# Decoder cells in a linear order beside each other, and channel gates made one chunk ahead of the routing

## The chip, the cores and the metric

The kernel runs on one core of a Trainium2 chip. A core has five engines with instruction streams of their own: TensorE (PE in the profile; its weight loads are listed apart as PEld), VectorE (DVE), ScalarE (ACT), GpSimd (POOL) and SyncE (SP), which mainly issues transfers. They work side by side and wait for each other through semaphores. The metric is the time of one execution on the device in microseconds (us), and of several executions the median.

## The reference

A tensor x of 8 sequences, 256 positions and 1024 features goes through three residual steps, each behind a layer norm. The first is a small decoder, which works at width 128 and has four layers; each layer is a recurrence along the 256 positions (written as a convolution by FFT in the reference) and a feedforward part. The second multiplies x by gates: for each sequence and feature, the 154 largest of 256 positions of a second input are marked, masked means and maxima over the positions are turned into gates by a 7-tap convolution, a batch norm and a sigmoid, and marked and unmarked positions get a gate each. The third is a mixture of 8 experts, two for each token. Cut to what matters (remarks behind # are added here):

```
def layernorm(x, w, b):                      # inside the decoder
    mu = jnp.mean(x, axis=-1, keepdims=True)
    var = jnp.mean((x - mu) ** 2, axis=-1, keepdims=True)
    return (x - mu) * jax.lax.rsqrt(var + EPS) * w + b
...
h = jnp.einsum('blv,dv->bld', x, Win) + bin  # 1024 -> 128
def body(h, p):                              # 4 layers
    l1w, l1b, pr, pi, lr, li, scl, l2w, l2b, w1, b1_, w2, b2_ = p
    y = jax.nn.silu(layernorm(h, l1w, l1b))
    y = sconv(y, pr + 1j * pi, lr + 1j * li) # complex exponential recurrence along the 256 positions
    h = h + y * scl
    y = layernorm(h, l2w, l2b)
    y = jax.nn.silu(jnp.einsum('bld,fd->blf', y, w1) + b1_)   # 128 -> 512
    y = jnp.einsum('blf,df->bld', y, w2) + b2_                # 512 -> 128
    return (h + y, None)
...
h = layernorm(h, lnl_w, lnl_b)
return jnp.einsum('bld,vd->blv', h, Wout) + bout              # 128 -> 1024
...
_, topk_idx = jax.lax.top_k(cm, k)           # k = 154 of 256, for each sequence and feature
mask = jnp.zeros((B, L, C), x.dtype).at[b_idx, l_idx, topk_idx].set(1.0)
...
return crucial_features * A_S1 + subcrucial_features * A_S2   # mask*x and (1-mask)*x, each gated
...
gate_logits = jnp.einsum('bsh,he->bse', x, gate_w)            # 8 experts
top_vals, top_idx = jax.lax.top_k(gate_logits, TOP_K)         # TOP_K = 2
...
expert_out = jnp.einsum('bsh,eho->bseo', x, expert_w)         # 1024 -> 1024
...
x = x + _L0_attn_ref(_layernorm(x, axis=-1), L0_attn_Win, ...
x = x + _L0_xattn_ref(_layernorm(x, axis=-1), ctx_4096, ...
x = x + _L0_ffn_ref(_layernorm(x, axis=-1), L0_ffn_gate_w, L0_ffn_expert_w)
return x
```

## The kernel before

The 2048 tokens are kept in the core's memory with features in the partitions, in four chunks (`NCH`) of 512 columns (`CT`), which are two sequences each. The kernel is written in Tile, a framework in which the program is plain Python and a scheduler fixes each engine's order of instructions when the kernel is built: it goes by the order in the program as priority, by what each instruction depends on, and by its own guess of durations, and may draw a later instruction ahead where an earlier one isn't ready by its guess. On the chip each engine then runs its list in that fixed order.

Five stages follow each other. **Decoder with threshold search** comes first. `start(c)` (L329 to L354) transposes a chunk (32 transposes, L337) for its statistics (L339) and multiplies it by Win (L348). A cell (l, c) is layer l for chunk c. Its first half is `recurrence` (L396 to L418): `inverse_std` squares on ScalarE (L382), sums by four narrow matmuls (L385), adds epsilon on VectorE (L388), takes the power on GpSimd (L390), and spreads it by four transposes (L137, in `over_features`); then VectorE normalizes (y, L399), ScalarE applies SiLU (L401), VectorE multiplies by the phases (mi, L405), runs four scans (L408) and multiplies again (L411), and TensorE adds the centered state (L413) and two matmuls with mi (L415) into one PSUM tile. Its second half is `feedforward` (L420 to L437): `inverse_std` on that tile, z on VectorE (L425), four matmuls with W1 (L429), four SiLUs on ScalarE (L432), four matmuls with W2 into the same PSUM tile (L435), and h on ScalarE (L437). After the last layer `put_out(c)` (L441 to L461) multiplies by Wout (eight matmuls, L458), adds to x (L459) and takes statistics for the next layer norm.

The order of cells is written at L464 to L504, in waves: wave w holds the cells with l + c = w, so that there are 1, 2, 3, 4, 3, 2 and 1 cells in the seven waves. All recurrences of a wave are written first, then the start of one more chunk, then all feedforwards of the wave:

```
cells = [(wave - c, c) for c in range(NCH) if 0 <= wave - c < DEPTH]
turned = [recurrence(l, c) for l, c in cells]
...
for (l, c), xc in zip(cells, turned):
    feedforward(l, c, xc)
```

The output weights are prepared in wave 3, and from that wave on each wave ends with `put_out`.

The search for the 154th largest value (L510 to L603) needs nothing from the decoder. It stands behind it in the program, so its instructions fill gaps. It has four parts of 16 rows: four trials of 16 Signs with a sum on ScalarE (L550), each followed by some nine small instructions on VectorE (L553 to L565); then for each of 16 rows three VectorE instructions (L571, L573, L574), small ones, and 16 comparisons that write the mask (L596). A branch (L606) for rows where the search failed follows; no engine goes past it before both the decoder and the search are done.

**Masked sums and maxima** (L632 to L650, VectorE and ScalarE) and **convolution and batch norm** (L679 to L750) come next. In **gating and routing** a loop over chunks (L893 to L908) makes four gates of four slices each on ScalarE (L902), adds the deviations and multiplies x on VectorE (L905, L907), and calls `route(c)` (L772 to L877): gate logits on TensorE (L779), transposes of the tokens to rows (L791), row statistics, normalized rows stored to memory, two experts picked of eight (sel, L826; wt, L827, L831), ranks within each expert (L839, L841), a payload (pay, L874) and eight scatters on GpSimd (L877). **Experts** comes last: the slots' tokens are gathered (L968), transposed (L940), multiplied by the expert's weights (L950), weighted and added into the output by indirect transfers (L991).

PSUM has three kinds of tiles of 128 x 512 in the decoder: tp in two buffers (transposes, W1 results, Wout results), mm in four (a cell's state), st in two (statistics). In the routing the pool is another one: st in two buffers and a tile of double size, x2, in two.

Of the kernel before, what the change touches and what calls it, by code (L numbers as in the profile page):

```python
# [8 lines left out]
F32 = mybir.dt.float32  # L9
# [6 lines left out]
P = 128  # L16
# [39 lines left out]
def decoder_kernel(ctx: ExitStack, tc: tile.TileContext, x_t, ctx_t, vecs, win_t, w1_t, w2_t, wout_t,  # L56
# [8 lines left out]
    until_gates = ctx.enter_context(ExitStack())  # L65
    psum = until_gates.enter_context(tc.tile_pool(name="psum", bufs=2, space=bass.MemoryType.PSUM))

    def ps_tp():
        return psum.tile([P, CT], F32, tag="tp", name="ps_tp", bufs=2)

    def ps_mm():
        return psum.tile([P, CT], F32, tag="mm", name="ps_mm", bufs=4)

    def ps_st():
        return psum.tile([P, CT], F32, tag="st", name="ps_st", bufs=2)


    ident = const.tile([P, P], F32, name="ident")
# [70 lines left out]
    with ExitStack() as early:  # L149
        tkp = early.enter_context(tc.tile_pool(name="topk", bufs=1))  # L150

        with ExitStack() as dec:
# [243 lines left out]
            def recurrence(l, c):  # L396
                rb = inverse_std(h[c])
                y = lp.tile([P, CT], F32, tag="y", name="y")
                nc.vector.tensor_tensor(y, h[c], rb, ALU.mult)  # L399
                s = lp.tile([P, 2, S], F32, tag="s", name="s")  # L400
                nc.scalar.activation(s.rearrange("p a t -> p (a t)"), y, AF.Silu,  # L401
                                     bias=col("ln1_b", l), scale=col("ln1_w", l))

                mi = lp.tile([P, 2, 2, S], F32, tag="mi", name="mi", bufs=2)
                nc.vector.tensor_tensor(mi, both(s, 1), both(turn[:, l], 2), ALU.mult)  # L405
                for a, ini in enumerate((init_a, init_b)):
                    for q in range(2):
# [3 lines left out]
                nc.vector.tensor_tensor(mi, mi, both(turn[:, l], 2), ALU.mult)  # L411
                xc = ps_mm()
                nc.tensor.matmul(out=xc, lhsT=center, rhs=h[c], start=True, stop=False)  # L413
                for a in range(2):
                    nc.tensor.matmul(out=xc, lhsT=turned_w[:, l],  # L415
                                     rhs=mi[:, a].rearrange("p q t -> p (q t)"),
                                     start=False, stop=(a == 1))
                return xc  # L418
# [22 lines left out]
            def put_out(c):  # L441
# [18 lines left out]
                                           ALU.add)  # L460
                wide_inverse_std(xs[c], inv_std[:, at_c])  # L461


            for wave in range(DEPTH + NCH - 1):  # L464
                cells = [(wave - c, c) for c in range(NCH) if 0 <= wave - c < DEPTH]
                turned = [recurrence(l, c) for l, c in cells]
                if wave == 0:
                    phases(slice(1, DEPTH))
                if wave + 1 < NCH:
                    start(wave + 1)  # L470
                for (l, c), xc in zip(cells, turned):
                    feedforward(l, c, xc)
                if wave == NCH - 1:

                    wo = wp.tile([P, NK, DIM], F32, tag="w_io", name="wo")
                    nc.sync.dma_start(out=wo.rearrange("p k d -> p (k d)"), in_=wout_t)
                    bp = ps_st()
                    for k in range(NK):
                        nc.tensor.matmul(out=bp[:, k : k + 1], lhsT=wo[:, k, :], rhs=col("lnl_b"), start=True,
                                         stop=True)  # L480
                    v.tensor_tensor(bo, bo, bp[:, 0:NK], ALU.add)
                    wo_mean = wp.tile([P, 1], F32, name="wo_mean")
                    v.tensor_reduce(wo_mean, wo, AX.XY, ALU.add)
                    v.tensor_scalar(wo_mean, wo_mean, 1.0 / D, None, ALU.mult)
                    v.tensor_scalar(wo, wo, wo_mean, col("lnl_w"), ALU.subtract, ALU.mult)
                    v.tensor_tensor(wo_mean, wo_mean, col("lnl_w"), ALU.mult)
                    bp = ps_st()
                    nc.tensor.matmul(out=bp[:, 0:NK], lhsT=mean_x, rhs=bo, start=True, stop=True)
                    bo_mean = wp.tile([P, 1], F32, name="bo_mean")
                    v.tensor_reduce(bo_mean, bp[:, 0:NK], AX.X, ALU.add)  # L490
                    v.tensor_scalar(bo, bo, bo_mean, None, ALU.subtract)


                    for g in range(2):
                        o = slice(4 * g, 4 * g + 4)
                        om = ps_tp()
                        nc.tensor.matmul(out=om, lhsT=ones, rhs=wo[:, o, :].rearrange("p k d -> p (k d)"),
                                         start=True, stop=True)
                        off = lp.tile([P, CT], F32, tag="z", name="off")
                        v.tensor_scalar(off, om, 1.0 / DIM, 1.0 / DIM, ALU.mult, ALU.add)  # L500
                        v.tensor_tensor(wo[:, o, :].rearrange("p k d -> p (k d)"),
                                        wo[:, o, :].rearrange("p k d -> p (k d)"), off, ALU.subtract)
                if wave >= DEPTH - 1:
                    put_out(wave - DEPTH + 1)  # L504

# [170 lines left out]
    with tc.tile_pool(name="xattn", bufs=2) as cp:  # L676
# [408 lines left out]
```

## Time and profile before

| | |
|---|---|
| time, median of 3 runs | 1357.23 us (1355.61 to 1359.68) |
| profiled execution, its own time | 1359.86 us |
| its span | 1358.0 us |
| mean granted TensorE clock | 0.862 |
| set-up and first start, 0 to 36.8 us | 36.8 us |
| decoder and search, to 503.7 us | 466.9 us, TensorE busy 366.4, VectorE 317.3, ScalarE 255.5 |
| masked sums and maxima, to 577.0 us | 73.3 us, VectorE busy 66.4 |
| convolution and batch norm, to 590.5 us | 13.5 us |
| gating and routing, to 731.8 us | 141.3 us, TensorE busy 79.7, VectorE 78.6, ScalarE 74.1 |
| experts, to 1358.0 us | 626.2 us, TensorE busy 597.5 |

The profile is one execution with its instructions' start and end times. The span is from the first to the last of them; the execution's own time has a little more around it. An instruction's row gives its line in the kernel, the engine, the operation, output and input tiles by their names in the program, and shapes. What ended an idle time is inferred from the semaphores. TensorE's granted clock is given as a share of full speed. A 128 x 512 matmul of 32-bit numbers shows as two records.

### The profile page before, as it was taken

Reading aid. Unit: us, or ns where it says so; the run is one execution under the profiler, and the core shown is the slowest. Engines: PE = TensorE matmul, PEld = TensorE weight load, DVE = VectorE, ACT = ScalarE, POOL = GpSimd, SP = SyncE. Lnnn points to the kernel's source line nnn. Section 1 sums busy time; section 2 is a strip of 40 time slices with the busy share of each in tenths; the row PEclk is TensorE's granted clock in tenths of the full one; section 3 lists DMA queues with packets and bytes.
Section 4 is the critical chain, followed back from the end, with each engine's and each line's share of the span. In section 5 each row is a group of like instructions: output and inputs, shape, how many; then the busy total and the mean of one; then the engine's idle time right before and its main releaser. Section 6 shows DMA issues by size and latency. Waiting matters only on the chain. (4 is left out here: it accounts for less than half of the span.)

```text
span 1358.0 us, 10519 instructions
## 1 busy us (share of the span) xinstructions
PE 1079.4 (79%) x3197; PEld 543.8 (40%) x3197; DVE 555.7 (41%) x1716; ACT 441.0 (32%) x1148; POOL 212.1 (16%) x213
## 2 busy tenths in 40 slices
PE   6778787987959661055663999999999999999996
PEld 4434344444434231023341444444444444444442
DVE  7771878387486769956651001000100010001000
ACT  0158565853847415956630000000000000000000
POOL 1021112101110010002323112111211112111100
PEclk9788787986979775557665999999999999999998
DMA  9100001001000000003375254362636253452622
GB/s 382 69 1 1 1 15 63 1 0 38 25 0 1 0 1 17 1 31 142 139 237 181 62 141 109 80 197 62 186 78 201 62 160 92 100 175 62 162 40 33
DMA packets 39203, 113.66 MB, mean 84 GB/s; under 512 B 4244, under 2 KB 4836, under 8 KB 37860
## 3 DMA queue, kind: packets, MB, share of 16 engines
q0 software_dynamic: 12544, 41.98, 14.3%
q1 hardware_dynamic: 23810, 62.44, 12.6%
q10 hardware_dynamic: 2786, 8.51, 1.6%
q8 instruction: 27, 0.44, 0.1%
q14 instruction: 36, 0.29, 0.1%
HBM read 74.57 MB, written 38.35 MB: 83 GB/s over the span
## 5 line engine op out<-in xcount | busy, mean ns | idle before, releaser
L950 PE MATMUL ps_mm<-w,xT 128*128 128x512 f32 x1280 | 561.2, 596 | 10.9 <-ACT xT L942 10.9
L950 PEld LDWEIGHTS ps_mm<-w,xT 128*128 128x128 f32 x1280 | 240.4, 190 | 308.2 <-issue 287.7
L990 DVE TENSOR_SCALAR y<-ps_mm,wgt 128x512 f32<-128x512 f32 x40 | 30.0, 751 | 544.5 <-PE ps_mm L950 530.9
L991 POOL DMA_INDIRECT out_dram<-y,to x40 | 63.1, 1577 | 497.3 <-DVE xT L944 415.7
L550 ACT ACTIVATE tkj<-ctx,tk_trial 128x256 f32<-128x256 f32 x256 | 129.1, 504 | 26.3 <-DVE tk_trial L565 17.1
L988 ACT ACTIVATE y<-ps_mm,wgt 128x512 f32<-128x512 f32 x40 | 27.5, 687 | 292.0 <-PE ps_mm L950 292.0
L942 ACT COPY xT<-ps_tp 128x512 f32<-128x512 f32 x40 | 23.4, 585 | 277.5 <-PE ps_tp L940 277.5
L390 POOL TENSOR_TENSOR rs<-ve,minus_half 128x4 f32<-128x4 f32 x36 | 42.5, 1182 | 245.5 <-DVE ve L388 223.6
L429 PE MATMUL ps_tp<-z,w 128*128 128x512 f32 x128 | 76.5, 726 | 3.5 <-DVE z L425 3.2
L415 PE MATMUL ps_mm<-mi,turned_w 128*128 128x512 f32 x64 | 48.8, 908 | 31.9 <-DVE mi L411 31.8
L137 PE MATMUL ps_st<-ident,rs 128*128 128x128 f32 x160 | 32.2, 333 | 41.0 <-POOL rs L390 41.0
L649 ACT ACTIVATE comb<-comb 128x256 f32<-128x256 f32 x128 | 51.5, 404 | 25.0 <-DVE smax L646 24.4
L435 PE MATMUL ps_mm<-f,w 128*128 128x512 f32 x128 | 59.4, 595 | 0.0
L432 ACT ACTIVATE f<-ps_tp,b1f 128x512 f32<-128x512 f32 x64 | 43.6, 683 | 27.4 <-PE ps_tp L429 26.9
L385 PEld LDWEIGHTS ps_st<-mean_w,sq 128*128 128x128 f32 x288 | 43.6, 228 | 11.7 <-ACT sq L382 7.3
L940 PEld LDWEIGHTS ps_tp<-ident,src 128*128 128x128 f32 x320 | 38.1, 143 | 25.5 <-issue 20.6
L550 ACT ACTIVATION_READ_ACCUMULATOR tkj<-ctx,tk_trial 128x1 f32 x256 | 48.1, 188 | 0.0
L940 PE MATMUL ps_tp<-ident,src 128*128 128x128 f32 x320 | 42.4, 276 | 4.8 <-DMA src<-normed_rows,to 4.8
L968 POOL DMA_INDIRECT src<-normed_rows,to x40 | 42.0, 1050 | 20.0 <-issue 11.6
L385 PE MATMUL ps_st<-mean_w,sq 128*128 128x1 f32 x288 | 42.2, 268 | 3.1 <-ACT sq L382 3.1
L429 PEld LDWEIGHTS ps_tp<-z,w 128*128 128x128 f32 x128 | 28.2, 233 | 40.0 <-issue 24.9
L877 POOL DMA_INDIRECT meta<-pay,at x32 | 34.4, 1074 | 59.8 <-DVE pay L874 51.2
(325 smaller groups left out, 1278.2 us busy)
## 6 DMA issues: line engine op xcount, KB each, us to landing
w<-in_expert_w_dram SPq DMA_DIRECT2D x32, 1024.0 KB, 7.6
x<-in_x_t_dram SPq DMA_DIRECT2D x8, 1024.0 KB, 15.8
ctx<-in_ctx_t_dram SPq DMA_DIRECT2D x16, 512.0 KB, 6.3
out_dram<-row ACTq DMA_DIRECT2D x16, 512.0 KB, 2.7
normed_rows<-normed SPq DMA_DIRECT2D x16, 512.0 KB, 2.6
w<-in_w_t_dram SPq DMA_DIRECT2D x2, 1024.0 KB, 12.3
src<-normed_rows,to POOLq DMA_INDIRECT x40
out_dram<-y,to POOLq DMA_INDIRECT x40
```

What stands on the lines that cost most here:

```text
L385: nc.tensor.matmul(out=st[:, q : q + 1], lhsT=sq[:, q * P : (q + 1) * P], rhs=mean_w, start=True, stop=True)
L390: nc.gpsimd.tensor_tensor(rs, ve, root, ALU.pow)
L415: nc.tensor.matmul(out=xc, lhsT=turned_w[:, l], rhs=mi[:, a].rearrange("p q t -> p (q t)"), start=False, stop=(a == 1))
L429: nc.tensor.matmul(out=fps, lhsT=w1[:, l, f * P : (f + 1) * P], rhs=z, start=True, stop=True)
L432: nc.scalar.activation(ft, fps, AF.Silu, bias=b1[:, 4 * l + f : 4 * l + f + 1])
L435: nc.tensor.matmul(out=xc, lhsT=w2[:, l, f, :], rhs=ft, start=False, stop=(f == DFF // P - 1), skip_group_check=True)
L550: nc.scalar.activation(junk, ctx_h[:, i, :], AF.Sign, bias=trial[:, 0, i : i + 1], accum_out=trial[:, 1, i : i + 1])
L649: nc.scalar.activation(comb[:, st, :], comb[:, st, :], AF.Copy, accum_out=ssum[:, st, b, k : k + 1])
L940: nc.tensor.transpose(tp[:, k * P : (k + 1) * P], src[:, kk * P : (kk + 1) * P], ident)
L950: nc.tensor.matmul(out=op, lhsT=xT[:, k * P : (k + 1) * P], rhs=ws[2 * g + k // KH][:, k % KH, :], start=(k == 0), stop=(k == NK - 1))
L968: nc.gpsimd.indirect_dma_start(out=src, out_offset=None, in_=normed_rows, in_offset=bass.IndirectOffsetOnAxis(ap=to[:, j : j + 1], axis=0) ...
L991: nc.gpsimd.indirect_dma_start(out=out, out_offset=bass.IndirectOffsetOnAxis(ap=to[:, j : j + 1], axis=0), in_=y, in_offset=None, bounds_c ...
```

## The change

The decoder's loop no longer goes by waves. Its 16 cells stand in a list, layer by layer and chunk by chunk within a layer. Step n writes the recurrence of cell n and then the feedforward of cell n-1, so that a recurrence always stands beside the feedforward of the chunk in front of it. The starts of chunks 1 to 3 stand in steps 0 to 2, the output weights (the same work, now in a function `weights_out`) in step 4, and `put_out` follows the feedforward of a chunk's last layer. PSUM's tp gets three buffers, mm three, st two.

In gating and routing, the gates of a chunk become a function `gated(c)`. Those of chunk 0 are written first, then, for each chunk, those of the next one and its own `route`. st has four buffers there. For the experts the counts go back to 2, 4 and 2. The number of instructions of each kind and the data that they work on stay the same. In the changed file the decoder's lines are 2 higher and later ones 9 or more (L415 is L417, L779 is L788, L902 is L911).

```
@@ -65
+    tp_bufs, mm_bufs, st_bufs = 3, 3, 2
...
-        return psum.tile([P, CT], F32, tag="tp", name="ps_tp", bufs=2)
+        return psum.tile([P, CT], F32, tag="tp", name="ps_tp", bufs=tp_bufs)
...
-        return psum.tile([P, CT], F32, tag="mm", name="ps_mm", bufs=4)
+        return psum.tile([P, CT], F32, tag="mm", name="ps_mm", bufs=mm_bufs)
...
-        return psum.tile([P, CT], F32, tag="st", name="ps_st", bufs=2)
+        return psum.tile([P, CT], F32, tag="st", name="ps_st", bufs=st_bufs)
@@ -460
-            for wave in range(DEPTH + NCH - 1):
-                cells = [(wave - c, c) for c in range(NCH) if 0 <= wave - c < DEPTH]
-                turned = [recurrence(l, c) for l, c in cells]
-                if wave == 0:
+            def weights_out():
+
+                wo = wp.tile([P, NK, DIM], F32, tag="w_io", name="wo")
...
+                return wo, wo_mean, bo_mean
+
+
+            cells = [(l, c) for l in range(DEPTH) for c in range(NCH)]
+            turned = []
+            for n in range(len(cells) + 1):
+                if n < len(cells):
+                    turned.append(recurrence(*cells[n]))
+                if n == 0:
                     phases(slice(1, DEPTH))
-                if wave + 1 < NCH:
-                    start(wave + 1)
-                for (l, c), xc in zip(cells, turned):
-                    feedforward(l, c, xc)
-                if wave == NCH - 1:
...
-                if wave >= DEPTH - 1:
-                    put_out(wave - DEPTH + 1)
+                if n + 1 < NCH:
+                    start(n + 1)
+                if n == NCH:
+                    wo, wo_mean, bo_mean = weights_out()
+                if n > 0:
+                    l, c = cells[n - 1]
+                    feedforward(l, c, turned[n - 1])
+                    if l == DEPTH - 1:
+                        put_out(c)
@@ -888
         until_gates.close()
+        st_bufs = 4
         psum = until_sorted.enter_context(tc.tile_pool(name="psum_rows", bufs=2, space=bass.MemoryType.PSUM))
-        before = None
-        for c in range(NCH):
+        def gated(c):
...
@@ -905
                     nc.vector.tensor_tensor(gate, gate, sb[:, o].unsqueeze(1).to_broadcast([P, 4, S]), ALU.add)
                     x2 = xs[c][:, 4 * g : 4 * g + 4, o]
                     nc.vector.tensor_tensor(x2, x2, gate, ALU.mult)
+
+        before = None
+        gated(0)
+        for c in range(NCH):
+            if c + 1 < NCH:
+                gated(c + 1)
             before = route(c, before)
...
     until_sorted.close()
+    tp_bufs, mm_bufs, st_bufs = 2, 4, 2
```

More of the change, by code (lines that the diff above doesn't have):

```diff
@@ L461, in put_out @@
                 wide_inverse_std(xs[c], inv_std[:, at_c])
-            for wave in range(DEPTH + NCH - 1):
-                cells = [(wave - c, c) for c in range(NCH) if 0 <= wave - c < DEPTH]
-                turned = [recurrence(l, c) for l, c in cells]
-                if wave == 0:
-                    phases(slice(1, DEPTH))
-                if wave + 1 < NCH:
-                    start(wave + 1)
-                for (l, c), xc in zip(cells, turned):
-                    feedforward(l, c, xc)
-                if wave == NCH - 1:
[L475 to L502, printed above, removed]
-                if wave >= DEPTH - 1:
-                    put_out(wave - DEPTH + 1)
@@ new lines, in weights_out @@
+            def weights_out():
+                wo = wp.tile([P, NK, DIM], F32, tag="w_io", name="wo")
+                nc.sync.dma_start(out=wo.rearrange("p k d -> p (k d)"), in_=wout_t)
+                bp = ps_st()
+                for k in range(NK):
+                    nc.tensor.matmul(out=bp[:, k : k + 1], lhsT=wo[:, k, :], rhs=col("lnl_b"), start=True,
+                                     stop=True)
+                v.tensor_tensor(bo, bo, bp[:, 0:NK], ALU.add)
+                wo_mean = wp.tile([P, 1], F32, name="wo_mean")
+                v.tensor_reduce(wo_mean, wo, AX.XY, ALU.add)
+                v.tensor_scalar(wo_mean, wo_mean, 1.0 / D, None, ALU.mult)
+                v.tensor_scalar(wo, wo, wo_mean, col("lnl_w"), ALU.subtract, ALU.mult)
+                v.tensor_tensor(wo_mean, wo_mean, col("lnl_w"), ALU.mult)
+                bp = ps_st()
+                nc.tensor.matmul(out=bp[:, 0:NK], lhsT=mean_x, rhs=bo, start=True, stop=True)
+                bo_mean = wp.tile([P, 1], F32, name="bo_mean")
+                v.tensor_reduce(bo_mean, bp[:, 0:NK], AX.X, ALU.add)
+                v.tensor_scalar(bo, bo, bo_mean, None, ALU.subtract)
+                for g in range(2):
+                    o = slice(4 * g, 4 * g + 4)
+                    om = ps_tp()
+                    nc.tensor.matmul(out=om, lhsT=ones, rhs=wo[:, o, :].rearrange("p k d -> p (k d)"),
+                                     start=True, stop=True)
+                    off = lp.tile([P, CT], F32, tag="z", name="off")
+                    v.tensor_scalar(off, om, 1.0 / DIM, 1.0 / DIM, ALU.mult, ALU.add)
+                    v.tensor_tensor(wo[:, o, :].rearrange("p k d -> p (k d)"),
+                                    wo[:, o, :].rearrange("p k d -> p (k d)"), off, ALU.subtract)
+                return wo, wo_mean, bo_mean
```

## The prediction

> **What bounds the kernel now.** I read the page's 40 slices first, then busy time by window, and only then the waits inside the two windows that the change touches.
>
> ```profile
> PE   6778787987959661055663999999999999999996
> DVE  7771878387486769956651001000100010001000
> PEclk9788787986979775557665999999999999999998
> ```
>
> A slice is 34 us. From slice 22 on TensorE is full: the experts, 626 us that the change leaves alone. Before that no engine is full. The windows give the decoder with the threshold search and the gating with the routing:
>
> ```profile
> 36.80:503.70 466.90, 366.37 (x1148) 194.59 (x1147) 317.26 (x922) 255.45 (x681) 62.17 (x62) 0.82 0.04 13
> 590.50:731.80 141.30, 79.74 (x289) 43.20 (x288) 78.61 (x272) 74.09 (x121) 38.51 (x36) 0.64 0.46 157
> ```
>
> Columns: window, length, busy PE, weight load, VectorE, ScalarE, GpSimd, granted clock. TensorE is busy 366 of 467 us in the first, at clock 0.82; its idle time is next (us, times, longest):
>
> ```profile
> PE ps_st L137 <- POOL rs L390: 41.0, 27, 2.5
> PE ps_mm L415 <- DVE mi L411: 31.8, 7, 7.4
> PE ps_tp L337 <- DVE bn L339: 8.7, 4, 3.9
> ```
>
> Two dependences inside a cell hold 73 of about 100 us: the power on GpSimd between statistics and transposes, and the recurrence on VectorE ahead of L415. TensorE's timeline shows one recurrence and its feedforward back to back, nothing between them to fill with:
>
> ```profile
> 449.51 0.65 PE L137 MATMUL ps_st<-ident,rs 128*128 128x128 f32 x4 [1.41 <-POOL rs L390]
> 457.02 3.78 PE L415 MATMUL ps_mm<-mi,turned_w 128*128 128x512 f32 x4 [6.86 <-DVE mi L411]
> 461.48 1.05 PE L385 MATMUL ps_st<-mean_w,sq 128*128 128x1 f32 x8 [0.69 <-ACT sq L382]
> 464.26 0.65 PE L137 MATMUL ps_st<-ident,rs 128*128 128x128 f32 x4 [1.72 <-POOL rs L390]
> 466.31 6.32 PE L429 MATMUL ps_tp<-z,w 128*128 128x512 f32 x8 [1.40 <-DVE z L425]
> 472.46 3.60 PE L435 MATMUL ps_mm<-f,w 128*128 128x512 f32 x8
> ```
>
> (Eight records of 3.60 us in L435 are four matmuls.) In the routing, the first transposes of chunks 1 to 3 stand 30.7 us apart, each behind VectorE work of the chunk before:
>
> ```profile
> 624.56 1.94 PE L791 MATMUL ps_x<-ident,x 128*128 128x128 f32 x8 [2.74 <-DVE wt L827]
> 655.31 1.94 PE L791 MATMUL ps_x<-ident,x 128*128 128x128 f32 x8 [3.14 <-DVE wt L831]
> 678.53 0.60 PE L839 MATMUL ps_st<-sel,upper 128*128 128x8 f32 x2 [5.77 <-DVE sel L826]
> 686.10 1.94 PE L791 MATMUL ps_x<-ident,x 128*128 128x128 f32 x8 [3.14 <-DVE wt L831]
> ```
>
> VectorE also carries the threshold search, whose end the branch awaits with the decoder's (busy, mean ns; idle before):
>
> ```profile
> L571 DVE TENSOR_SCALAR_CACHE_REDUCE hid<-ctx,tk_t 128x256 f32<-128x256 f32 x64 | 30.5, 477 | 1.6
> L574 DVE MAX8 tk_m<-hid 128x8 f32<-128x256 f32 x64 | 27.2, 425 | 1.4
> L573 DVE SCALAR_TENSOR_TENSOR hid<-hid,ctx 128x256 f32<-128x256 f32 x64 | 27.0, 422 | 1.7
> L596 DVE TENSOR_SCALAR mask<-ctx,tk_t 128x256 uint8<-128x256 f32 x64 | 18.6, 344 | 0.0
> ```
>
> **What the Trainium skill says.** "TensorE: Matmul & The Clock Gate", "What's actually happening": an idle window of about 3.4 us halves the array's clock, as long a busy one restores it. The trace agrees in kind: an L415 record, behind the longest waits, takes 908 ns, an L435 record, never behind one, 595. So waits cost twice. "Perfetto Trace Analysis", "Tensor Engine Instruction": ScalarE and VectorE run strictly in order, TensorE draws only weight loads ahead. So the order fixed at build time decides; VectorE's waits of 8.1 us for the search's Signs (4 times) fit. "PSUM — Partial Sum Buffer", "Specifications": 8 banks of 2 KiB. 3+3+2 single tiles fill them, as do 4 and two double ones in the routing; no trace shows it.
>
> **Part 1, the decoder.** Work at full clock, per cell: a 128x512 matmul takes 0.86 us from its first record's start to the next matmul's; 8 of the feedforward, one centering and two of L415 make 9.5; statistics 2×0.81 and transposes 2×0.45, 2.5; with issue gaps 12.4, times 16 cells 198. Three starts of 11.6, four output parts of 16.6 and the output weights' 3.5 add 105: 303 us. The stage is 303 + 99.5 idle + 64 of slow clock (366 busy less 303).
>
> The built order of the changed kernel has TensorE repeat: L417(n) (the old L415), feedforward transposes of n−1, statistics and transposes of recurrence n+1, then 4 W1 and 4 W2 matmuls of n−1. The 8.1 us of matmuls lie where y .68, Silu .81, products 1.21, four scans 2.92, products 1.21 (6.86 with overlaps) ran uncovered; the feedforward's statistics come a step earlier, so their power is covered. A step is 12.95 us plus up to 1 of L417's wait: 13.8. Nothing is removed from any engine, and the extra tp buffer only lets a W1 matmul or output column run one ahead. Two mm tiles live at once need 2 of the 3.
>
> TensorE's end: first feedforward done about 97 (the start is the same); one step with start(3) to 128; two with the output weights to 161; eight of 13.8 to 271; four with an output part (22.5 to 26 as before, and 13.8): 36+41+41+36 to 425; 12 more for L417 waits and slow clock that I can't rule out, chosen between 0 and the 41 of a wait-by-wait account: **437** (425 to 466) against about 503.
>
> The branch comes later than that. In the old order VectorE has 3 search instructions after its last decoder instruction; in the new one 77: the last trial's Signs stand among the last squares, then come about 2 us of small ones, 16 triples of 1.45 (477+82+425+422 and gaps) = 23.2, 2.7 more, 16 masks of .29 = 4.7, .5: 33, of which 2 overlap. Branch at 437+31 = **468**, gain **36** (10 to 50). What was hidden in the slack is late next.
>
> **Part 2, gates ahead.** ScalarE makes 32 gate slices, not 16, first: 16 × .5 ends at 606.5; VectorE's add and multiply (1.21+1.21 a gate) end at 611. The first chunk's selection comes at 619.3, not 617.6: 1.7 lost. Then VectorE's 9.7 us of gates no longer stand between one chunk's selection and the next one's logits. A chunk: gate logits (L788, the old L779) 8.9, copy .6, eight row copies 5.2, statistics .9, power and mean 1.5, selection 1.7, rank 3.4 = 22.2, not 30.7. Three periods: 92 − 66.6 − 1.7 = **23** (14 to 29). GpSimd's 8 scatters take 10.2 to 11 a chunk and fit; payload, fetch and gathers follow the last selection as before (6 us to the payload). The two more st buffers free the rank matmul of a chunk from the next one's transposes: inside that 22.2. If the gates' 9.7 us still held the chain, the gain would be about 0.
>
> **Queues.** The expert weight loads on SP stand among the stores of normalized rows, not after them. Their transfers need no engine on the path and the last payload is later than any of them; at worst a store starts one 1 MB load later (7.6 us), which the 16 us from the last selection to the fetch cover.
>
> Sum: span 1358.0 − 36 − 23 = 1299; the profiled execution took 1359.86, 1.9 over its span and 2.6 over the median of 1357.23: 1300.9 profiled, about 1298 to 1300 as median. I take **1300**.
>
> **Rivals.** (1) The search's tail takes the decoder's gain: VectorE's 317 us don't get done faster because TensorE does, and the tail grows by the 35 saved. For: the 77 instructions; against: VectorE waits 65.6 us for TensorE's statistics before, and 317 in 431 us is 74%. Only the gates gain: 1335. (2) The gates gain nothing, the period being held by ScalarE's 74 us or the chain of ranks: 1322. For: ScalarE makes gates and rows; against: it is idle half of the window. (3) Slower: VectorE's fixed order puts search instructions, held by 16 Signs of .69 (11 us), ahead of y, the products and z, so L417 waits in each step, and each wait brings the slow clock back. Break-even is 59 us over 14 steps, 4.2 us a step; at 5 us, 70 us lost: 1369. For: the linear order has one cell in flight where waves had up to four, so a hold-up has less to hide behind. Against: such waits were 8.1 us in the whole stage. (4) The scheduler restores the old order and nothing moves: the built order speaks against it.
>
> **Chances.** Both parts work, 1282 to 1318: 0.62. (1) 0.15, (2) 0.09, (3) 0.11, (4) 0.03. Up to 1336 the first three are in; 1278 takes both parts near their upper ends. Left out: (3), (4) and 0.06 of tails. A difference under 0.3%, about the spread of the runs before, can't be told from none: faster 0.86, same 0.03, slower 0.11.
>
> **What would show it.** TensorE's waits for the power on GpSimd below 15 us (41 before) and for the recurrence's products (L413 in the new numbering) below 15 (31.8); clock near 0.9 in the decoder; the last output matmul at 425 to 466, the branch some 31 us later with VectorE in triples; first transposes of chunks 22 us apart. Waits of L417 above 4 us a step, or VectorE waiting long for tkj, make me wrong; so does a stretch over 45 us of VectorE alone ahead of the branch.

## The result and the profile after

The changed kernel takes 1340.73 us (median of 1338.79 to 1343.73) against 1358.45 for the kernel before on the same chip: ratio 0.9869, 95% interval 0.9837 to 0.9902. It is faster by 18 us, where 57 were forecast, and lies above the range. The profiled span is 1341.9 us against 1358.0, 16.1 less.

The 40 slices of the page of after, to be laid under those of before:

```profile
PE   6888799897777801056735999999999999999996
DVE  7864588787385389978720100010000100001000
PEclk8777989988687855558766999999999999999998
```

A hole has appeared in TensorE's row in slice 14 (counted from 0), where VectorE is busy. The busy times of the stretch up to it and of the hole itself (window, length, busy PE, weight load, VectorE, ScalarE, GpSimd, clock) show what it is:

```profile
36.80:469.20 432.40, 360.12 (x1141) 192.62 (x1140) 288.29 (x828) 255.51 (x681) 59.72 (x61) 0.85 0.04 14
469.20:497.50 28.30, 0.00 (x0) 0.02 (x1) 26.53 (x92) 0.00 (x0) 1.01 (x1) 0.51 0.00 0
```

TensorE ends at 469.2, some 34 us earlier than before; then VectorE alone finishes the search for 28.3 us, and the branch comes at 497.5, some 6 us earlier than before. In the kernel before, TensorE's last transposes and the branch stood together:

```profile
502.56 0.40 PE L185 MATMUL ps_st<-ident,line 1*128 1x1 f32 x4 [1.00 <-DVE line L182]
503.70 0.19 PE L603 MATMUL ps_st<-ones,bad 128*1 128x1 f32 x2 [0.74 <-DVE bad L601]
```

TensorE's waits in the changed kernel from 36 to 513 us, in the order of the page:

```profile
PE ps_st L139 <- POOL rs L392: 30.3, 24, 2.3
PE ps_st L612 <- DVE bad L610: 28.3, 1, 28.3
...
PE ps_mm L417 <- DVE mi L413: 3.2, 1, 3.2
```

The wait for the recurrence's products is gone as forecast (31.8 before, 3.2 now). The wait for the power on GpSimd is not: 41.0 has become 30.3, where I had said below 15. And the clock rose from 0.82 to 0.85 only: of the 360 us that TensorE is busy, 57 are more than the 303 of my sum for full clock (63 before), which I put down to slow clock.

In the routing, the first rank matmul of each chunk marks its selection:

```profile
613.73 1.02 PE L848 MATMUL ps_st<-sel,upper 128*128 128x8 f32 x4 [4.58 <-DVE sel L835]
...
638.09 0.59 PE L848 MATMUL ps_st<-sel,upper 128*128 128x8 f32 x2 [5.86 <-DVE sel L835]
...
663.27 0.60 PE L848 MATMUL ps_st<-sel,upper 128*128 128x8 f32 x2 [4.79 <-DVE sel L835]
...
689.76 0.60 PE L848 MATMUL ps_st<-sel,upper 128*128 128x8 f32 x2 [6.30 <-DVE sel L835]
...
714.60 0.43 PE L979 MATMUL ps_st<-ident,filled 40*128 40x40 f32 x2 [20.83 <-DMA filled<-meta]
```

Periods of 24.4, 25.2 and 26.5 us (29.9, 30.8 and 31.0 before), not 22.2. From the last selection to the fetched slots it is 24.8 us, 2.5 more than before. The stage, from the first transposes of the deviations at 584.46 to this fetch, is 130.1 us against 141.5. So the span's 16.1 are 5.8 from what precedes the routing, 11.4 from the routing, and 1.1 lost in the experts.

### The profile page after: what moved, and what is told of

Read it like the earlier page. It is cut to its first block, busy times and chain, and to the rows that moved or that the text cites. A ratio compares the mean times of both kernels' runs of the same rounds, so it can differ in the third digit from the quotient of the medians.

```text
span 1341.9 us, 10523 instructions
## 1 busy us (share of the span) xinstructions
PE 1072.7 (80%) x3197; PEld 540.9 (40%) x3197; DVE 555.0 (41%) x1716; ACT 440.7 (33%) x1148; POOL 211.0 (16%) x213
## 5 line engine op out<-in xcount | busy, mean ns | idle before, releaser
L431 PE MATMUL ps_tp<-z,w 128*128 128x512 f32 x128 | 73.1, 724 | 5.4 <-DVE z L427 5.4
L437 PE MATMUL ps_mm<-f,w 128*128 128x512 f32 x128 | 57.5, 592 | 0.0
L139 PE MATMUL ps_st<-ident,rs 128*128 128x128 f32 x160 | 30.1, 319 | 30.3 <-POOL rs L392 30.3
L387 PEld LDWEIGHTS ps_st<-mean_w,sq 128*128 128x128 f32 x288 | 40.1, 212 | 13.1 <-ACT sq L384 10.2
L431 PEld LDWEIGHTS ps_tp<-z,w 128*128 128x128 f32 x128 | 28.9, 236 | 40.5 <-issue 32.4
L387 PE MATMUL ps_st<-mean_w,sq 128*128 128x1 f32 x288 | 39.1, 256 | 5.9 <-ACT sq L384 5.9
L339 PE MATMUL ps_tp<-ident,x 128*128 128x128 f32 x128 | 25.7, 358 | 19.0 <-DVE bn L341 8.2
## 6 DMA issues: line engine op xcount, KB each, us to landing
x<-in_x_t_dram SPq DMA_DIRECT2D x8, 1024.0 KB, 11.4
ctx<-in_ctx_t_dram SPq DMA_DIRECT2D x16, 512.0 KB, 10.8
```

What stands on the lines that cost most here:

```text
L387: nc.tensor.matmul(out=st[:, q : q + 1], lhsT=sq[:, q * P : (q + 1) * P], rhs=mean_w, start=True, stop=True)
L431: nc.tensor.matmul(out=fps, lhsT=w1[:, l, f * P : (f + 1) * P], rhs=z, start=True, stop=True)
L437: nc.tensor.matmul(out=xc, lhsT=w2[:, l, f, :], rhs=ft, start=False, stop=(f == DFF // P - 1), skip_group_check=True)
```

## Experiments

### Each part alone

The changed decoder with the old gate loop, and the old waves with the new gate loop (each with the PSUM counts that belong to it).

```
e1:  (decoder as changed; until_gates.close() and after)
-        st_bufs = 4
+        tp_bufs, mm_bufs, st_bufs = 2, 4, 2
...
-        def gated(c):
+        before = None
+        for c in range(NCH):
e2:  (decoder as before)
+        st_bufs = 4
...
-        before = None
-        for c in range(NCH):
+        def gated(c):
```

> The linear order of cells alone, with the gates made as before. Theory A (the threshold search ends last, and the order of cells moves it little): the branch stays at about 497 us, 6 us earlier than before, though the last output part ends at 469; gain 5 to 8 us, ratio 0.994 to 0.997. Theory B (the two parts share one gain, the gates being worth nothing alone): gain near the full 17 us, ratio 0.987.

> The gates made one chunk ahead alone, with the waves as before. Theory A: the two parts stand in separate stages and add up: gain 10 to 12 us, ratio 0.991 to 0.993, periods between the chunks' selections of 24 to 27 us. Theory B (gates worth nothing alone): ratio 1.000. If the expert weights' loads were not the cause of the long last period, it would be 22 us here as forecast, and the gain 20.

Measured: 0.9956 (0.9940 to 0.9973) for the order of cells, 0.9904 (0.9868 to 0.9939) for the gates; the product is 0.9860, within the interval of the whole. The parts stand in separate stages and add up, within these intervals. The order of cells gives 6 us, the gates some 13. In the gates' own profile the stage takes 124.0 us, with periods of 24.4, 25.2 and 22.1: the first two are as in the changed kernel, the last one is as short as forecast. Single profiles differ by some us: the same waves bring the branch at 503.7 us in the profile of before and at 495.2 in that of e2, the linear order at 497.5 in the changed kernel and at 496.9 in e1.

### The decoder without the search

In both kernels the search is left out; the mask instructions stay. Each ran once.

```
-            st = small("st", 6)
-            for i in range(GH):
-                v.bn_stats(st[:, i, :], ctx_h[:, i, :])
...
+            t = small("t")
+            nc.gpsimd.memset(t, 0.0)
+            nc.gpsimd.memset(fails[:, hb : hb + 1], 0.0)
             for i in range(GH):
                 b, j = divmod(hb * GH + i, NK)
```

> The kernel before without the threshold search: the mask is a comparison with zero, the statistics, the trials and the triples are left out, the 64 mask instructions are kept. It shows where the waves end without the search beside them. Theory A (the search sets the branch): the last output part ends 20 to 40 us earlier than the 503 us of before. Theory B (the decoder's own dependences set it): it stays within 10 us of 503.

> The changed kernel without the threshold search, left out in the same way. Theory A: the branch comes right after the last output part, at 430 to 440 us as my own sum had it, 60 us earlier than in the changed kernel and 30 or more earlier than in the waves without the search; the last steps with an output part take 36 to 41 us, not 41 to 49. Theory B (the output parts are serial by themselves): these steps stay at 41 to 49 us and the last output part ends at 455 to 469.

The last transposes of the last output part and the branch's matmul on TensorE's timeline, in the waves:

```profile
488.70 0.40 PE L185 MATMUL ps_st<-ident,line 1*128 1x1 f32 x4 [0.77 <-DVE line L182]
489.03 0.19 PE L544 MATMUL ps_st<-ones,bad 128*1 128x1 f32 x2
```

and in the linear order:

```profile
469.88 0.40 PE L187 MATMUL ps_st<-ident,line 1*128 1x1 f32 x4 [0.77 <-DVE line L184]
470.22 0.19 PE L553 MATMUL ps_st<-ones,bad 128*1 128x1 f32 x2
```

The waves' branch comes 14 us earlier than the 503.7 of before, between the two theories and only 6 earlier than in e2's profile of the same waves. The linear order gains nothing: TensorE ends at 470 without the search, at 469 with it. So VectorE's and ScalarE's search costs the new order of cells no time on TensorE that shows, and theory A of e4, which had put 30 us of delay on it, falls. What remains of the search is its 28 us behind TensorE's end. With no search the linear order ends 19 us before the waves, not the 66 that I gave TensorE's end.

### Where the output parts are written

A look at one step with an output part in the changed kernel says where the missing time sits. TensorE's timeline of after:

```profile
300.61 3.60 PE L437 MATMUL ps_mm<-f,w 128*128 128x512 f32 x8
305.89 1.12 PE L415 MATMUL ps_mm<-h,center 128*128 128x512 f32 x2 [1.68 <-ACT h L439]
306.90 1.05 PE L387 MATMUL ps_st<-mean_w,sq 128*128 128x1 f32 x8
309.42 1.12 PE L139 MATMUL ps_st<-ident,rs 128*128 128x128 f32 x4 [1.47 <-POOL rs L392]
311.38 1.86 PE L451 MATMUL ps_st<-wo_mean,z 128*128 128x1 f32 x8 [0.85 <-DVE z L448]
...
314.98 9.40 PE L460 MATMUL ps_tp<-zm,wo 128*128 128x512 f32 x16 [0.78 <-DVE zm L455]
324.22 7.21 PE L181 MATMUL ps_st<-sq,mean_x 128*128 128x512 f32 x16
332.20 0.40 PE L187 MATMUL ps_st<-ident,line 1*128 1x1 f32 x4 [0.77 <-DVE line L184]
...
335.45 0.65 PE L139 MATMUL ps_st<-ident,rs 128*128 128x128 f32 x4 [1.86 <-POOL rs L392]
...
338.40 1.11 PE L139 MATMUL ps_st<-ident,rs 128*128 128x128 f32 x4 [1.41 <-POOL rs L392]
340.91 6.66 PE L431 MATMUL ps_tp<-z,w 128*128 128x512 f32 x8 [1.40 <-DVE z L427]
```

The output part (L451 to L187) runs with no cell's matmuls in it. It works on the state that the feedforward has just made, so ahead of it stands a chain of its own: from the end of the feedforward's matmuls (L437) at 304.2 us, the new state, centering, squares, statistics, power, transposes and z follow one behind the other, 10.8 us to the first matmul with Wout (L460). When the output part is over, the next recurrence's and the next feedforward's statistics follow, each with its wait for the power, and four W1 matmuls take 6.66 us instead of 3.6, at a slow clock.

In the waves three, two, one and no feedforward of other chunks stood between a chunk's last feedforward and its output part. In the second of these four, before's timeline shows the output part's statistics (L449) between another cell's matmuls:

```profile
356.69 0.95 PE L449 MATMUL ps_st<-wo_mean,z 128*128 128x1 f32 x8
...
359.58 3.60 PE L435 MATMUL ps_mm<-f,w 128*128 128x512 f32 x8
...
364.06 1.98 PE L458 MATMUL ps_tp<-zm,wo 128*128 128x512 f32 x4 [0.78 <-DVE zm L453]
```

Only 0.9 us pass there between the last of those matmuls and the first with Wout. For the four output parts these times are 7.5, 0.9, 6.0 and 9.5 us in the waves, 24 in sum, and 10.8, 10.2, 9.8 and 9.8 in the changed kernel, 41 in sum, where no feedforward stands between. Written one step later, an output part comes after the next feedforward and recurrence:

```
-            for n in range(len(cells) + 1):
+            for n in range(len(cells) + 2):
...
-                if n > 0:
-                    l, c = cells[n - 1]
-                    feedforward(l, c, turned[n - 1])
-                    if l == DEPTH - 1:
-                        put_out(c)
+                if 0 < n <= len(cells):
+                    feedforward(*cells[n - 1], turned[n - 1])
+                if n > 1 and cells[n - 2][0] == DEPTH - 1:
+                    put_out(cells[n - 2][1])
```

Once without the search, once with it where the change has it:

> The linear order with each output part written one step later, and the threshold search left out (mask compared with zero), so that nothing but the decoder is seen; to be set against the changed order without the search, whose last output part ended at 470 us with steps of 48 us. Theory A (the output parts are serial because of where they are written): steps with an output part fall to 35 to 40 us, the last ends at 440 to 450. Theory B (they are serial by their own chain of statistics): steps stay at 45 or more, the end at 465 or later.

> The changed kernel with each output part written one step later, the search behind the decoder as in the change. Theory A (the search's own pace, some 22 us a trial in the fixed order, sets the branch): the last output part ends near 450, the branch stays at 490 to 498, gain over the changed kernel under 7 us, ratio to before 0.982 to 0.988. Theory B (the search follows the decoder's end by 28 us whatever that is): branch at 478, ratio 0.973.

Without the search, TensorE ends at 446 instead of 470; steps with an output part end 42, 33 and 25 us apart. So the 24 us were the place in the program. With the search the kernel takes 1314.24 us: ratio 0.9704 (0.9686 to 0.9721), well clear of the change's 0.9869. TensorE's timeline from the feedforward ahead of the first output part (the last two rows are the last transposes and the branch):

```profile
316.19 3.60 PE L437 MATMUL ps_mm<-f,w 128*128 128x512 f32 x8
...
321.00 1.05 PE L451 MATMUL ps_st<-wo_mean,z 128*128 128x1 f32 x8 [0.78 <-DVE z L448]
...
323.32 8.56 PE L460 MATMUL ps_tp<-zm,wo 128*128 128x512 f32 x16 [0.78 <-DVE zm L455]
...
347.99 6.43 PE L431 MATMUL ps_tp<-z,w 128*128 128x512 f32 x8
...
438.34 0.40 PE L187 MATMUL ps_st<-ident,line 1*128 1x1 f32 x4 [0.77 <-DVE line L184]
475.03 0.19 PE L611 MATMUL ps_st<-ones,bad 128*1 128x1 f32 x2 [36.28 <-DVE bad L609]
```

TensorE's end falls to 439, the branch to 475. The expectation that the search's own pace would hold the branch at 490 or later was wrong: its instructions are laid between the decoder's, so it is drawn along, and keeps a tail of 28 to 36 us.

The two timelines say where the 30 us from 469 to 439 lie; up to the thirteenth feedforward (304.2 and 304.0 us) they agree. From the matmuls ahead of an output part to its first one with Wout pass 3.5, 4.2, 2.1 and 7.4 us, 17 in sum where it was 41. The output parts from there on take 5 us less in sum. The last three feedforwards, with the recurrences beside them, take 51 us in sum where they took 53: the cell behind the first output part still waits for the power and has W1 at 6.43 us. So what the late place saves is the output part's own chain ahead of it, and hardly anything in the cell behind it.

The run without the search ends 7 us later than the one with it, since its thirteenth feedforward ends at 313.6, not 304.0: the steps ahead are built in another order there. A few us between kernels with and without the search are therefore no price of the search.

### The search earlier

If the tail is only a matter of order, the search can be written earlier: its four parts as a function called in steps 3, 6, 9 and 12 (e5; with the late output parts, e7), all in step 12 (e11), or in 32 pieces, two a step (e12).

```
e5, e7:
+                if n in (3, 6, 9, 12):
+                    search((3, 6, 9, 12).index(n))
e11:
+                if n == 12:
+                    for hb in range(PARTS):
+                        search(hb)
e12:
+                if n >= 1:
+                    for _ in range(2):
+                        next(units, None)
```

> The changed kernel with the search's four parts written between the decoder's steps 3, 6, 9 and 12 instead of behind the decoder, so that they come earlier in VectorE's and ScalarE's order; no work is added or left out. Theory A (the decoder ends at 470 whatever the search does, and the search's tail of 28 us behind it is only a matter of order): the branch moves from 497 to about 471, the kernel to about 1314 us, ratio to before 0.968 to 0.974. Theory B (the search costs the decoder VectorE time when it comes earlier): the last output part moves back to 485 or later, and the kernel stays at 1330 to 1340 us, ratio 0.98 to 0.99.

> As the kernel with the search between the steps, and each output part written one step later, so that it stands beside a recurrence and a feedforward instead of ahead of them. Theory A (the output parts are serial because everything written after them takes its statistics tiles after them): a step with an output part falls from 41 to 49 us to about 38, the last output part ends 15 to 25 us earlier, at 445 to 455, ratio to before 0.955 to 0.965. Theory B (TensorE's work at a slow clock and the waits inside the output part set it): no difference to the kernel with the search between the steps, 0.97.

> Output parts one step later, and the whole search written at step 12, ahead of the last layer's steps only. Theory A (early search steals VectorE from the recurrence; late search leaves a tail; a place between gives both up): the middle steps stay at 14.5 us, the last output part ends at 455 to 470, the branch within 20 us of it, 1320 to 1330 us, ratio 0.972 to 0.980. Theory B: like the kernel with the search at steps 3 to 12, ratio 0.977, or worse.

> Output parts one step later, and the search cut into 32 pieces (a trial, or four rows of three VectorE instructions), two written behind each step from 1 on. Theory A (runs of 16 rows, 23 us of VectorE ahead of a recurrence's products, made the steps of 27 us in the kernel with four whole parts between the steps): no step above 18 us, last output part at 450 to 460, no tail, ratio 0.955 to 0.965. Theory B (VectorE's and ScalarE's sum of work is what lengthens them): the same as with whole parts, 0.977.

Measured: e5 0.9979 (0.9963 to 0.9995), e7 0.9766 (0.9740 to 0.9793), e11 0.9704 (0.9683 to 0.9725), e12 0.9740 (0.9724 to 0.9756). In e5 the tail is gone, and TensorE's end has moved from 469 to 513. Its waits say why:

```profile
PE ps_st L139 <- POOL rs L392: 31.6, 25, 2.4
PE ps_mm L417 <- DVE mi L413: 30.3, 6, 10.0
PE ps_tp L431 <- DVE z L427: 15.0, 6, 10.3
```

The wait for the products is back at 30 us, in pieces of up to 10. This is my rival (3), brought about by the edit: search instructions stand ahead of the products on VectorE. In the wait of 10.0 us that ends at 215.5, the four scans stand among them, and twelve mask instructions (3.2 us) just ahead of the products. Cutting the search into pieces leaves 20.8 us of it (e12). At step 12 the tail shrinks from 36 to 21 us and TensorE ends 15 later (454): the branch stays at 475. Theory B holds for e5 in kind, with a ratio worse than its 0.98 to 0.99, and neither wide nor narrow pieces make an early search free: TensorE ends at 481 in e7 and at 488 in e12, where theory A had 445 to 460. Against e5, e7 again shows the late output parts: 2% by themselves.

### PSUM counts

```
-    tp_bufs, mm_bufs, st_bufs = 3, 3, 2
+    tp_bufs, mm_bufs, st_bufs = 2, 4, 2
```

> The changed kernel with the old PSUM counts in the decoder (2, 4, 2 instead of 3, 3, 2). I costed the third tp buffer at nothing: ratio to the kernel before stays at 0.985 to 0.989. If the third tp buffer carried the gain, the W1 matmuls wait for ScalarE's SiLU and the last output part ends 10 us later or more, but with a tail that shrinks: ratio 0.987 to 1.0.

Measured: 0.9905 (0.9877 to 0.9932), as much as the gates alone give. On its timeline the last output part and the branch are later than in the changed kernel by 10 and 6.5 us:

```profile
478.68 0.40 PE L187 MATMUL ps_st<-ident,line 1*128 1x1 f32 x4 [2.27 <-DVE line L184]
504.02 0.19 PE L612 MATMUL ps_st<-ones,bad 128*1 128x1 f32 x2 [24.93 <-DVE bad L610]
```

So in the profiles the third tp buffer, which I had costed at nothing, is worth about what the decoder's part brings in the changed kernel; the linear order's other profiles, e1 and e6, have the branch at 496.9 and 495.9, the two of the waves at 503.7 and 495.2, so even this is no more than likely. The times alone can't tell it: the interval overlaps the change's (0.9837 to 0.9902). How the buffer acts isn't shown either. TensorE's W1 matmuls wait for ScalarE's SiLU for only 0.3 us here; the wait for the power is 34.3 us for 30.3, and the cells' matmuls are laid in another order.

### The output weights' step

Steps 3 and 4 took 43.5 us, 10 more than forecast; step 4 prepares the output weights. Moved to step 9 (with the late output parts):

```
-                if n == NCH:
+                if n == 9:
                     wo, wo_mean, bo_mean = weights_out()
```

> Output parts one step later, and the output weights prepared in step 9, not 4. Theory A (in step 4 the preparation's VectorE work stretched the recurrence's chain, which left TensorE waiting and slow: a step of 27 us): the third and fourth feedforwards end 14 us apart, not 27, one later step grows by 5 or less; last output part at 430, ratio to before 0.963 to 0.968 if the search's tail does not grow. Theory B (the preparation costs its 10 us wherever it stands): the pause moves to step 9, ratio 0.970 as without the move.

Measured: 0.9757 (0.9733 to 0.9780), slower than without the move. The third and fourth feedforwards are 14 us apart as theory A says, not 27, but three later ones of 18 to 23 us appear, and TensorE ends at 446, not 439. Theory B is nearer, though its 0.970 was too good: the preparation takes its time wherever it stands, and the steps around it are laid differently. Step 4 was no bad place.

### The gates and the row stores

What stretches the periods: half of the gates' VectorE work left out, and, apart from it, more buffers for the normalized rows. The last run joins the buffers to the move of the output weights.

```
e14:
-                    nc.vector.tensor_tensor(gate, gate, sb[:, o].unsqueeze(1).to_broadcast([P, 4, S]), ALU.add)
e6, e15, e16:
-                xn = ep.tile([P, D], F32, tag="normed", name="normed", bufs=2)
+                xn = ep.tile([P, D], F32, tag="normed", name="normed", bufs=4)
```

> Output parts one step later, and the gates without the addition of the deviation (one VectorE instruction of 1.21 us a gate left out, half of the gates' VectorE work, 4.9 of 9.7 us a chunk; the gates' values change). Theory A (the gates made ahead still stand before the row statistics on VectorE, and stretch the periods between selections from 22.2 to 24.4 and 25.2 us): the first two periods fall by 2 to 3 us each, to 22 or 23; the first selection comes 2.4 to 5 us earlier. Theory B (TensorE's logits at slow clock and the rank's matmuls set the periods): they stay at 24.4 and 25.2.

> The changed kernel with four buffers for the normalized rows, not two. Theory A (ScalarE stood 11 us behind a row store that queued behind expert weights, and so delayed the last chunk's logits and rows): the wait goes, the last two periods between selections shrink from 25.2 and 26.5 to 22 to 24 us, gain over the changed kernel 4 to 8 us, ratio to before 0.981 to 0.984. Theory B (the periods are set by TensorE's logits and VectorE, as in the first one with 24.4): no change, ratio 0.987.

> Output parts one step later and four buffers for the normalized rows. Theory A (the row stores behind expert weights hold ScalarE only in some executions, where the last period is 26.5 us rather than 22): the profile's routing stays at 124 us, no gain that can be told, ratio 0.967 to 0.971. Theory B (the buffers save 5 us each time): 0.966 or less.

> All three: output parts one step later, output weights in step 9, four buffers for the normalized rows. If the parts add up: ratio 0.960 to 0.967; if the search's tail takes what the output weights give: 0.968 to 0.971.

Without the addition (e14, one run) the first selection comes 2.5 us earlier in the stage and the first two periods are 22.1 and 24.2, not 24.4 and 25.2. So the gates still stand ahead of the row statistics on VectorE, for 2.3 us in the first period and 1.0 in the second. But the last period is 30.1, since ScalarE stands still for 15.6 us at a normalized row. In the changed kernel the same wait is 11.3 us; its ScalarE timeline:

```profile
676.48 1.24 ACT L820 ACTIVATE normed<-row,ts_nm,ts_rs 128x1024 f32<-128x1024 f32 x1 [11.28 <-DMA normed_rows<-normed]
...
682.44 0.56 ACT L791 COPY lline<-ps_st 8x512 f32<-8x512 f32 x1
```

and SyncE's queue just before:

```profile
654.98 2.48 SPq L943 DMA_DIRECT2D w<-in_expert_w_dram  x3
662.83 1.47 SPq L821 DMA_DIRECT2D normed_rows<-normed  x2
```

Three loads of 1 MB of expert weights go out ahead of two row stores of 0.5 MB; the first of them, issued at 662.8, has landed only when ScalarE goes on at 676.5 (median of the last four stores: 6.6 us), the two buffers are not free, and the last chunk's row and logit copies stand behind the third row on ScalarE. Four buffers take that wait away (e6: none left, last period 22.7, stage 124.3). In time this cannot be told from the changed kernel: 0.9864 (0.9839 to 0.9890). Nor does it show with the late output parts, 0.9719 (0.9691 to 0.9746) against 0.9704: there the last period is 21.7 with two buffers and 22.5 with four. As to time, theory A of e15 holds. But the wait is there with two buffers each time: it was 9.6 us in e10 and 9.5 in e2, whose last periods are 21.7 and 22.1, 11.3 in the changed kernel (26.5) and 15.6 in e14 (30.1). The shorter waits cost nothing, the longer ones stretch the period. e16 gives 0.9742 (0.9719 to 0.9765): the parts do not add up, and the late output parts alone stay the fastest.

## Why the prediction was right in direction and wrong in size

**Right.** Faster, by both parts, in separate stages. The recurrence's products no longer hold TensorE (3.2 us). The steady step: 14.5 us measured (from 177.3 to 293.3 for eight) against 13.8. The tail behind TensorE's end: 28.3 against 31. The first selection: 1.7 us later, as worked out. Rivals (2), (3) and (4) did not come.

**Wrong: TensorE's end, 469 for 437.** The terms, in the order of the sum: first feedforward 98.6 for 97; step with the third start to 133.8 for 128; two steps with the output weights 43.5 for 33; eight steps 116 for 110; four with an output part 176 for 154; allowance 12 used up. The step that failed most is "36+41+41+36" (its own figures give 36.3 to 39.8 a step, not 41). It took output parts at the 22.5 to 26 us that they had before, where other chunks' feedforwards had covered part of their chain; in the changed kernel none does, and from the end of the feedforward's matmuls to the last transposes they take 27 to 29 us, 112 in sum; by the same count it was 18 to 27 in the waves, 93 in sum. The cells were taken at 13.8; two of them, behind an output part, take 20. Moved by one step, the same work ends at 439 (446 without the search). That this is close to the 437 of the sum is in part chance: the first output part is reached 19 us later than in the sum, and the allowance of 12 and shorter output steps make up for it.

**Wrong: the wait for the power and the clock.** I let the wait fall below 15 and the clock rise to 0.9. 72 us of idle time and 57 of slow clock remain in the changed kernel, 129 where the sum left 97. With late output parts they are 56 and 43 (401.9 us to TensorE's end, 345.8 of them busy).

**Wrong, by the profiles: the third tp buffer at nothing.** Without it TensorE's end is 10 us later and the branch 6.5. I named no work that hid it; what it does stays open.

**Wrong in size: the gates, 11 to 17 us for 23.** Their stage takes 130.1 us in the changed kernel's profile and 124.0 with the gates alone. The forecast's period of 22.2 left out that gates made ahead still come before the row statistics of the same period: 24.4 and 25.2, of which e14 shows 2.3 and 1.0. The rest of the second period's excess stays open. The "Queues" step said that a store may start one load later, under cover of the 16 us after the last selection. The store that mattered was one of the chunk before the last, and ScalarE, not the fetch, waited for it.

**Rival (1)** gave 1335, near the measured 1341, but not by its mechanism: the tail was 28.3 us, below the 31 forecast and not 35 more, and TensorE was late. Had the search held the branch, an earlier end of TensorE would have left it where it was; with late output parts it moved from 497 to 475. A number that fits is no evidence for its story.

## What to carry to other kernels

In a software pipeline written by hand, price each odd piece of work (a prologue, an output part, a preparation) with the chain that leads to it from the result it needs, and ask what runs beside that chain: here four output parts, written directly behind the feedforward whose result they need, cost 24 to 30 us of TensorE's end, more than the whole change brought. Filler work on a second engine, written last, ended after the first one here; moving it forward pays only if it does not come ahead of the critical chain on its own engine, since the order there is fixed. And a buffer count that a change touches is a step of the sum of its own.

## What the runs showed of the hardware

The length of one wait does not tell whether TensorE's clock falls. In the changed kernel it fell in a wait of 1.45 us amid narrow matmuls and transposes (timeline; the four W1 matmuls of L431 take 3.6 us at full clock). A wait of 2.32 us, 16 us earlier and amid the same kind of work, had left it full:

```profile
252.97 0.65 PE L139 MATMUL ps_st<-ident,rs 128*128 128x128 f32 x4 [2.32 <-POOL rs L392]
253.46 3.60 PE L431 MATMUL ps_tp<-z,w 128*128 128x512 f32 x8
...
266.86 0.95 PE L387 MATMUL ps_st<-mean_w,sq 128*128 128x1 f32 x8
269.26 1.11 PE L139 MATMUL ps_st<-ident,rs 128*128 128x128 f32 x4 [1.45 <-POOL rs L392]
270.17 1.71 PE L387 MATMUL ps_st<-mean_w,sq 128*128 128x1 f32 x8
271.74 5.40 PE L431 MATMUL ps_tp<-z,w 128*128 128x512 f32 x8
```

The same eight records of L387 take 0.95 us before the short wait and 1.71 behind it, and L431 5.40; the granted clock is 1.00 from 267 to 268 and 0.50 from 269 to 275. In e1 the same instructions with the same wait of 2.32 us went the other way:

```profile
248.01 0.65 PE L139 MATMUL ps_st<-ident,rs 128*128 128x128 f32 x4 [2.32 <-POOL rs L392]
248.50 5.29 PE L431 MATMUL ps_tp<-z,w 128*128 128x512 f32 x8
```

There the transposes right behind the wait still ran at full clock (0.65 us), and the granted clock fell more than a microsecond later, with TensorE busy: 1.00 to 249, 0.70 from 249 to 250, then 0.50. So the clock can be lost to a stretch of thin work with short waits, none of which decides alone, where the Trainium skill ("TensorE: Matmul & The Clock Gate", "What's actually happening") speaks of an idle window of some 3.4 us; no wait in these stretches was that long. Whether the narrow matmuls count as idle there was not tried.
